# Layer 3 of a four-layer network: scores of two token tiles by seven half-size products, and gathered rows weighted by ScalarE and added by one VectorE operation

## The chip, the cores and the metric

The kernel runs on one core of a Trainium2 chip. The metric is the time of one execution on the device in microseconds, the median of three runs before the change. One execution was also taken by the hardware profiler; all times of single instructions come from that one. The core's engines are TensorE (PE; its weight loads are listed apart as PEld), VectorE (DVE), ScalarE (ACT), GpSimd (POOL) and SyncE (SP). Each works through its own instructions in order, and they wait for one another through semaphores.

## The reference, cut to what matters

Four layers work on an array x of 4 images, 512 channels and 32 × 32 = 1024 tokens each; layers 0 to 2 are attention, a channel gate and attention again. The change lies in layer 3 and in the last step of layer 2. Layer 3 looks every token up in a memory of 2048 rows of 512 values:

```python
q = jnp.transpose(x, (0, 2, 3, 1)).reshape(-1, C)     # x: normalised in groups of channels
att = q @ mempool.T                                   # 4096 tokens x 2048 rows
vals, idx = jax.lax.top_k(att, k)                     # k = 8
vals = jax.nn.softmax(vals, axis=1)
att_sparse = jnp.zeros_like(att).at[rows, idx].set(vals)
out = att_sparse @ mempool                            # sum of 8 weighted rows
x = x + out                                           # (from_tokens)
```

All is float32.

## The kernel before, in words

The tokens of layer 3 are cut into 32 tiles of 128 tokens, eight per image, in the list `tiles`. A tile passes three functions, each a step later than the one before, in the loop `for s in range(end + 3)`:

- `attention` (L1512) multiplies the tile's normalised tokens, `xn3[b]`, with the transposed memory `memT` (four blocks of 128 channels by 2048 rows). It does so in two halves of 1024 rows; each half is 8 products of 128 × 128 by 128 × 512 that add over the four channel blocks in one pair of PSUM banks, which `next_pair` hands out in turn from three. ScalarE copies each half into `att` in SBUF (L1526).
- `pick` (L1531) finds the eight largest scores (`vector.max`, shown as MAX8) and their places (`max_index`, shown as MATCH_VALUE_LOAD and FIND_INDEX8), lets GpSimd gather the eight memory rows of each token with eight indirect DMAs into `got` (128 tokens × 8 rows × 512), and makes the exponentials `et` and their sum on ScalarE. SyncE loads the tile's old x into `xr`. There are three buffers `got`, under the tags q, k and v.
- `read` (L1586) divides `et` by the sum and adds the eight weighted rows on VectorE: one `tensor_scalar_mul` (L1591) and seven `scalar_tensor_tensor` (L1593). TensorE then turns the result to channels by four transposes (L1598), into one of two PSUM banks.

`put` (L1601), a step later, adds the result to `xr` and sends it out. The last two tiles take another way, `read_last` (L1572): TensorE multiplies the gathered rows with diagonal matrices of the weights.

Instructions wrapped in `pin` keep the order in which they are written on their engine. So VectorE works, per tile, through MAX8, FIND_INDEX8, `put` of an older tile, the weights and the eight weighted additions, and GpSimd's gathers of a tile follow its FIND_INDEX8.

`prepare3` loads and normalises the next image's tokens during an image's later tiles; odd images lie in the first part of `o_full`, even ones in `xn`. `put_out2` (L1466) is the last step of layer 2 for the last image: four projections on TensorE, which stand between `attention` of tile 0 and `attention` of tile 1; VectorE adds each projection to the old x and takes its statistics, ScalarE scales the old x before that.

Layers 0 to 2 already form products by seven half-size products in `seven`, with the helpers `add7` and `sub7` (L1048), through which all their sums go.

Of the kernel before, what the change touches and what calls it, by code (L numbers as in the profile page):

```python
# [41 lines left out]
def fast_net(ctx: ExitStack, tc: tile.TileContext, a: dict, out: bass.AP, flag: bass.AP):  # L42
# [13 lines left out]
    def pin(ins):  # L56

        return tc.keep_in_program_order(ins)
# [131 lines left out]
    def tokens(src):  # L190
        return lambda k, n: src[:, k, n * NB:(n + 1) * NB]

    def project(w, rhs, m, at, evacuate, name="proj"):


        ps = place(at, f"{name}_{m}")
        for n in range(T // NB):
            for k in range(KC):
                pin(nc.tensor.matmul(  # L199
                    ps[:, n, :], w[:, k, m * P:(m + 1) * P], rhs(k, n),  # L200
                    start=(k == 0), stop=(k == KC - 1),
                ))
        evacuate(flat2(ps))
# [1259 lines left out]
        nc.vector.tensor_mul(  # L1463
            I["o"][:, m, n * NB:(n + 1) * NB], I.pop(("pv", m, n)), I.pop(("rb", m, n)))

    def put_out2(b):  # L1466
        I = img[b]
        s1 = l2[b][1]
        mv = small.tile([P, KC, 2], F32, tag="mv", name=f"mv_d{b}")

        def add_out(m, ps):
            st = small.tile([P, 2, 6], F32, tag="bnst", name=f"st_d{b}_{m}")
            for n in range(T // NB):
                xr = apool.tile([P, NB], F32, tag="xr", bufs=2, name=f"xr_c{b}_{m}_{n}")
                nc.sync.dma_start(out=xr, in_=x1[b][:, m, n * NB:(n + 1) * NB])
                pin(nc.scalar.activation(
                    xr, xr, AF.Identity, bias=I["tb"][:, m:m + 1], scale=s1[:, m:m + 1]))
                nc.vector.tensor_add(xr, ps[:, n * NB:(n + 1) * NB], xr)
                nc.sync.dma_start(out=x2[b][:, m, n * NB:(n + 1) * NB], in_=xr)
                nc.vector.bn_stats(st[:, n, :], xr)  # L1480
            nc.vector.bn_aggr(mv[:, m, :], st.rearrange("p i s -> p (i s)"))

        for m in range(KC):
            project(I["Wp"], tokens(I["o"]), m, None, lambda ps: add_out(m, ps), f"p2_{b}")
        gc3 = const.tile([P, 2, KC], F32, tag=f"gc3_{b}", name=f"gc3_{b}")
        l3[b] = (mv, gc3)

# [21 lines left out]
            ))  # L1509
            yield  # L1510

    def attention(b, tt, between=None):  # L1512

        nm = f"{b}_{tt}"
        att = eight_k([P, NI], f"att_{nm}")
        for i, (lo, hi) in enumerate(
                ((0, T), (T, T + NB), (T + NB, NI)) if (b, tt) == tiles[-1] else ((0, T), (T, NI))):
            sc = flat2(next_pair())
            for i0 in range(lo, hi, NB):
                for k in range(KC):  # L1520
                    pin(nc.tensor.matmul(  # L1521
                        sc[:, i0 - lo:i0 - lo + NB],
                        xn3[b][:, k, tt * P:(tt + 1) * P], memT[k][:, i0:i0 + NB],
                        start=(k == 0), stop=(k == KC - 1),
                    ))
            pin(nc.scalar.copy(att[:, lo:hi], sc[:, 0:hi - lo]))  # L1526
            if between is not None and i == 0:
                between()
        return att

    def pick(b, tt, att):  # L1531

        nm = f"{b}_{tt}"
        top = small.tile([P, TOPK], F32, tag="top", name=f"top_{nm}")
        if (b, tt) == tiles[-1]:
            tops = small.tile([P, 3, TOPK], F32, tag="tops", bufs=1, name="tops")
            for i, (lo, hi) in enumerate(((0, T), (T, T + NB), (T + NB, NI))):
                pin(nc.vector.max(tops[:, i, :], att[:, lo:hi]))
            pin(nc.vector.max(top, tops.rearrange("p i n -> p (i n)")))
        else:  # L1540
            pin(nc.vector.max(top, att))  # L1541
        ix = small.tile([P, TOPK], mybir.dt.uint32, tag="ix", name=f"ix_{nm}")
        pin(nc.vector.max_index(ix, top, att))
        got = big("qkv"[(b * TC + tt) % 3], f"got_{nm}").rearrange("p k (i c) -> p (k i) c", c=C)
        for i in range(TOPK):
            pin(nc.gpsimd.indirect_dma_start(  # L1546
                out=got[:, i, :], out_offset=None, in_=a["mem"],
                in_offset=bass.IndirectOffsetOnAxis(ap=ix[:, i:i + 1], axis=0),
                bounds_check=NI - 1, oob_is_err=False,
            ))  # L1550
        nmx = small.tile([P, 1], F32, tag="nmx", name=f"tmx_{nm}")
        pin(nc.vector.tensor_scalar_mul(nmx, top[:, 0:1], -1.0))  # L1552
        et = small.tile([P, TOPK], F32, tag="et", name=f"et_{nm}")
        rs = small.tile([P, 1], F32, tag="rs", name=f"trs_{nm}")
        nc.scalar.activation(et, top, AF.Exp, bias=nmx, scale=1.0, accum_out=rs)
        i = (b * TC + tt) % 3
        xr = eT_flat[:, i * NB:(i + 1) * NB].rearrange("p (k q) -> p k q", q=P)
        nc.sync.dma_start(out=xr, in_=x2[b][:, :, tt * P:(tt + 1) * P])
        return got, et, rs, xr

# [9 lines left out]
            pin(nc.scalar.activation(dg[:, i, :], ident, AF.Identity, scale=et[:, i:i + 1]))  # L1570
        return dg

    def read_last(b, tt, picked, dg):

        got, et, rs, xr = picked
        tp = next_bank().rearrange("p (k q) -> p k q", q=P)
        for i in range(TOPK):
            for m in range(KC):
                pin(nc.tensor.matmul(
                    tp[:, m, :], got[:, i, m * P:(m + 1) * P], dg[:, i, :],  # L1580
                    start=(i == 0 and m == 0), stop=(i == TOPK - 1),
                    skip_group_check=True,
                ))
        return tp, xr

    def read(b, tt, picked):  # L1586
        got, et, rs, xr = picked
        nm = f"{b}_{tt}"
        weigh(et, rs, nm)
        acc = apool.tile([P, NB], F32, tag="rb", bufs=2, name=f"acc_{nm}")  # L1590
        pin(nc.vector.tensor_scalar_mul(acc, got[:, 0, :], et[:, 0:1]))  # L1591
        for i in range(1, TOPK):
            pin(nc.vector.scalar_tensor_tensor(  # L1593
                acc, got[:, i, :], et[:, i:i + 1], acc, ALU.mult, ALU.add
            ))
        tp = next_bank().rearrange("p (k q) -> p k q", q=P)
        for m in range(KC):
            pin(nc.tensor.transpose(tp[:, m, :], acc[:, m * P:(m + 1) * P], ident))  # L1598
        return tp, xr

    def put(b, tt, done):  # L1601
        tp, xr = done
        pin(nc.vector.tensor_add(xr, tp, xr))
        nc.sync.dma_start(out=out_v[b, :, :, tt * P:(tt + 1) * P], in_=xr)
# [244 lines left out]
        places7[key] = nine[3 * i:3 * i + 3]  # L1849
    places7["Wq"] = places7["Wp"]  # L1850
    nc.gpsimd.tensor_scalar_mul(same, same, 8.0 / T)
    tiles = [(b, tt) for b in range(B) for tt in range(TC)]
    atts, picks, sums = {}, {}, {}
    scores2(0, UNITS2[0])
    for b in range(B):
# [29 lines left out]
            first7[2]()  # L1885
        apply2(b, UNITS2[-1])
        if last:
            atts[0] = attention(*tiles[0], lambda: invert2(b))
            finish2(b)
            put_out2(b)  # L1890
            continue
        over_keys(b, *UNITS2[-1][:2])
        at_border[0] = True
# [36 lines left out]
        nc.vector.tensor_scalar(  # L1930
            flag, tps[0:1, 0:1], float(2 * P * NS * B * (TC + 2 * KC)), None, ALU.not_equal)

    ahead, behind = iter(()), chain(behind, norm3(B - 1))
    end = len(tiles)
    diags = {}

    def pick_last(s):
        at = s - 1
        picks[at] = pick(*tiles[at], atts.pop(at))
        put(*tiles[s - 3], sums.pop(s - 3))  # L1940
        weigh(*picks[at][1:3], f"{tiles[at][0]}_{tiles[at][1]}")

    for s in range(end + 3):
        closing = end - 1 <= s <= end
        if closing:
            pick_last(s)
        if s < end:
            b, tt = tiles[s]
            if s > 0:
                atts[s] = attention(b, tt, (lambda: diags.update(  # L1950
                    {0: diagonals(0, picks[end - 2][1])})) if closing else None)
        if 0 <= s - 1 < end and not closing:
            picks[s - 1] = pick(*tiles[s - 1], atts.pop(s - 1))
        if s == end:
            diags[1] = diagonals(1, picks[end - 1][1])
        if s >= 3 and not closing:
            put(*tiles[s - 3], sums.pop(s - 3))
        if 0 <= s - 2 < end:
            at = s - 2
            sums[at] = (read(*tiles[at], picks.pop(at)) if at < end - 2  # L1960
                        else read_last(*tiles[at], picks.pop(at), diags[at - end + 2]))
        if s < end and tt == 2:
            ahead = prepare3(b + 1) if b + 1 < B else iter(())
        if s < end and tt >= 2:
            next(ahead, None)
        if s < end and 1 <= s <= TC:
            next(behind, None)
        if s == TC + 2:
            check_range()
        if s == TC + 4:  # L1970
            again = nc.values_load(flag, min_val=0, max_val=1)
    return again


# [702 lines left out]
```

## Time and profile before

| what | value |
|---|---|
| median of three runs | 2516.8 us (2515.85 to 2518.11) |
| the profiled execution's own time | 2516.74 us |
| its span, first to last instruction | 2514.7 us |
| TensorE busy | 2469.2 us, 98% |
| VectorE busy | 1824.1 us, 73% |
| ScalarE busy | 1026.0 us, 41% |
| GpSimd busy | 1226.5 us, 49% |
| attention of tile 1 on TensorE | 2051.7 to 2065.6 us |
| repeating part of layer 3 | 2065.7 to 2490.9 us |
| tail after the last score product | 2490.9 to 2514.7 us |

Lines of the profile are to be read so: a line of the timeline has start, duration, engine, source line, operation, output<-inputs, shapes, and in brackets how long the engine had been idle and what ended that. Consecutive instructions of one line are merged (x7). A line of windows has the stretch and its length, and then busy time and instruction count of PE, PEld, DVE, ACT and POOL, the granted clock of TensorE, and the share and rate of the DMA engines. A line of groups has count, busy time in us, mean ns of one instruction, and the idle time before.

### The profile page before, as it was taken

The numbers are of one execution on the slowest core, as the hardware profiler recorded it, in microseconds if no ns is written. First come the engines' busy times: TensorE is split into PE (matmuls) and PEld (weight loads), VectorE is DVE, ScalarE is ACT, GpSimd is POOL, SyncE is SP. The second block draws the span as 40 slices with busy tenths as digits, with TensorE's granted clock in tenths as the row PEclk, the third lists the DMA queues.
The fourth block names the chain that finished last, engine by engine and source line by source line (L and its number), as shares of the span: only waits on it lengthen the run. The fifth ranks groups of instructions, "written<-read, shape, count | busy, mean of one in ns | idle before, by whom it ended". The sixth has DMA issues, their size and how long they took to land.

```text
span 2514.7 us, 48075 instructions
## 1 busy us (share of the span) xinstructions
PE 2469.2 (98%) x18512; PEld 1171.9 (47%) x18512; DVE 1824.1 (73%) x2962; ACT 1026.0 (41%) x1245; POOL 1226.5 (49%) x1688
## 2 busy tenths in 40 slices
PE   9999999999999999999999999999999999999998
PEld 4344534555355534555633633453363344444445
DVE  5799568875788548886768677576757647887876
ACT  1567346652665336651353145125324512121212
POOL 3266425553465426554284247127405617566665
PEclk9999999999999999999999999999999999999999
DMA  2588348872698438893201230131113046667666
GB/s 85 157 229 230 111 131 224 244 215 85 176 243 232 138 89 216 238 247 125 97 30 68 103 128 18 63 116 40 55 50 134 26 135 191 214 191 219 183 188 179
DMA packets 190031, 367.19 MB, mean 146 GB/s; under 512 B 32985, under 2 KB 96473, under 8 KB 185570
## 3 DMA queue, kind: packets, MB, share of 16 engines
q1 hardware_dynamic: 109712, 186.58, 23.9%
q0 software_dynamic: 49152, 142.79, 21.0%
q10 hardware_dynamic: 30930, 34.66, 4.9%
q8 instruction: 149, 2.44, 0.4%
q14 instruction: 88, 0.72, 0.1%
HBM read 190.10 MB, written 39.58 MB: 91 GB/s over the span
## 4 chain that ended last, share of the span: by engine, by line
PE 68%; DMA 8%; issue 7%; POOL 7%; DVE 6%; ACT 3%; ACTq 0%; POOLq 0%; SPq 0%; DVEq 0%
PE pair L1121 12%; PE pair L1369 8%; PE pv L578 8%; POOL got L1546 6%; PE pair L199 6%; PE pair L513 6%; PE pair L539 5%; PE pt L471 5%; PE pt L1406 4%; PE pair L1247 4%; PE pv L1406 4%; DMA got<-in_mem,ix 4%; PE pt L767 3%; PE pair L1521 2%; ACT e L546 2%
## 5 line engine op out<-in xcount | busy, mean ns | idle before, releaser
L528 POOL DMA_DIRECT2D s<-ss x512 | 258.1, 511 | 398.2 <-issue 113.2
L552 DVE STREAM_TRANSPOSE eT<-e 128x1024 f32<-128x1024 f32 x256 | 316.4, 1236 | 161.4 <-ACT e L546 161.0
L1546 POOL DMA_INDIRECT got<-in_mem,ix x256 | 280.5, 1096 | 211.9 <-DVE tmx L1552 142.8
L1363 ACT ACTIVATE eT<-pair 128x1024 f32<-128x1024 f32 x256 | 248.5, 1022 | 312.5 <-PE pair L1369 188.9
L567 DVE BATCH_NORM_STATS2 st<-e 128x6 f32<-128x256 f32 x1024 | 350.8, 404 | 0.0
L1387 POOL TENSOR_TENSOR e<-eT 128x1024 f32<-128x1024 f32 x96 | 239.8, 2501 | 166.6 <-ACT eT L1363 122.2
L546 ACT ACTIVATE e<-pair 128x1024 f32<-128x1024 f32 x256 | 251.9, 1022 | 163.8 <-PE pair L539 122.1
L519 ACT COPY ss<-pair 128x1024 f32<-128x1024 f32 x256 | 248.9, 1019 | 85.4 <-DMA s<-ss 35.4
L513 PE MATMUL pair<-k,q 64*32 64x512 f32 x4096 | 267.3, 598 | 13.0 <-ACT e L546 13.0
L578 PEld LDWEIGHTS pv<-eT,v 128*64 128x64 f32 x4096 | 221.1, 137 | 71.6 <-issue 55.2
L578 PE MATMUL pv<-eT,v 128*64 128x128 f32 x4096 | 250.0, 275 | 4.1 <-ACT pv L638 4.1
L1369 PE MATMUL pair<-q,k 64*128 64x512 f32 x1024 | 240.0, 605 | 2.0 <-DVE sum L1048 0.9
L1388 DVE TENSOR_TENSOR eT<-eT,e 128x1024 f32<-128x1024 f32 x96 | 144.7, 1508 | 130.1 <-POOL e L1387 129.9
L539 PE MATMUL pair<-s,wmix 32*32 32x512 f32 x4096 | 160.6, 600 | 3.4 <-DMA s<-ss 1.9
L1593 DVE SCALAR_TENSOR_TENSOR acc<-got,et,acc 128x512 f32<-128x512 f32 x210 | 157.9, 752 | 7.5
L1383 POOL TENSOR_TENSOR eT<-eT 128x1024 f32<-128x1024 f32 x32 | 83.4, 2605 | 161.1 <-ACT eT L1363 156.2
L1369 PEld LDWEIGHTS pair<-q,k 64*128 64x128 f32 x1024 | 92.3, 186 | 140.2 <-issue 66.6
L1526 ACT COPY att<-pair 128x1024 f32<-128x1024 f32 (+1 forms) x65 | 64.9, 999 | 216.4 <-PE pair L1521 216.3
L513 PEld LDWEIGHTS pair<-k,q 64*32 64x32 f32 x4096 | 57.1, 105 | 178.6 <-ACT e L546 84.1
L1048 DVE TENSOR_TENSOR k<-k,pair 128x512 f32<-128x512 f32 (+1 forms) x96 | 78.1, 857 | 66.5 <-PE pair L1121 52.8
L651 POOL TENSOR_TENSOR o<-pv,rb 64x256 f32<-64x256 f32 x128 | 118.9, 929 | 6.4
L1541 DVE MAX8 top<-att 128x8 f32<-128x2048 f32 x31 | 71.1, 2293 | 70.0 <-ACT att L1526 70.0
(383 smaller groups left out, 3745.2 us busy)
## 6 DMA issues: line engine op xcount, KB each, us to landing
s<-ss SPq DMA_DIRECT2D x512, 128.0 KB
s<-ss POOLq DMA_DIRECT2D x512, 128.0 KB, 4.4
rb<-r POOLq DMA_DIRECT2D x64, 128.0 KB, 6.0
o<-o SPq DMA_DIRECT2D x32, 256.0 KB
xr_c<-x SPq DMA_DIRECT2D x32, 256.0 KB
rb_c<-r SPq DMA_DIRECT2D x64, 128.0 KB
eT<-x SPq DMA_DIRECT2D x32, 256.0 KB
out<-eT SPq DMA_DIRECT2D x32, 256.0 KB
```

Source lines behind the costliest of these rows:

```text
L513: pin(nc.tensor.matmul(sc[m * NS:(m + 1) * NS, r, :], q[r * HD:(r + 1) * HD, m, s * NS:(s + 1) * NS], k_[r * HD:(r + 1) * HD, m, n * NB:(n ...
L519: pin(nc.scalar.copy(ss[:, :, n * NB:(n + 1) * NB], sc))
L528: pin(relays[side].dma_start(out=s2[2 * m + r::NH], in_=ss[m * NS:(m + 1) * NS, r, :]))
L539: pin(nc.tensor.matmul(mixed(s, r // 2)[t * NS:(t + 1) * NS, r % 2, :].rearrange("p (qq k) -> p qq k", qq=2), wmix[r * NS:(r + 1) * NS], s ...
L546: pin(nc.scalar.activation(e[:, half].rearrange("p r qq k -> p (r qq k)"), flat2(mixed(s, half)), AF.Exp))
L552: pin(nc.vector.transpose(eT[:, j % 2].rearrange("p b (qq i r) x -> p i r qq b x", qq=2, i=4)[:, i, 2 * half:2 * half + 2], e[:, half].rea ...
L567: pin(nc.vector.bn_stats(st[:, i, 2 * half + r, qq, :], e[:, half, r, qq, :]))
L578: pin(nc.tensor.matmul(pv[r * HD:(r + 1) * HD, gp, :], I["v"][:, t, g * HD:(g + 1) * HD], eT[:, j % 2, t, :, 4 * g:4 * g + 4], start=(t == ...
L1121: pin(nc.tensor.matmul(ps[:, m, :], w[:, k, m * P:(m + 1) * P], x[:, k, :], start=(k == 0), stop=(k == 1)))
L1363: pin(nc.scalar.activation(e, scs[len(es)], AF.Exp, scale=SCALE))
L1369: pin(nc.tensor.matmul(sc[:, r, :], I["k"][r * HD:(r + 1) * HD, m, t * P:(t + 1) * P], I["q"][r * HD:(r + 1) * HD, m, n * NB:(n + 1) * NB] ...
L1546: pin(nc.gpsimd.indirect_dma_start(out=got[:, i, :], out_offset=None, in_=a["mem"], in_offset=bass.IndirectOffsetOnAxis(ap=ix[:, i:i + 1], ...
```

## The change

The tiles of an image are taken in pairs, tokens tt and tt + 4 (`tiles` is reordered). For a pair, the scores are a matrix of 2 × 2 blocks: two tiles by two halves of the memory, over two halves of the channels. `two_tiles` makes them by seven products of half the channels each, 28 multiplications of 128 × 128 by 128 × 512 in place of 32. Three of the results add in PSUM onto an earlier one after ScalarE has copied that out; three are added to `att` by VectorE. The products need sums of memory blocks, `memory_sums`, made once on VectorE during `put_out2`, and sums of token blocks, `token_sums`, made for each pair. This is done for tiles 2 to 29; tiles 0, 1, 30 and 31 go by `attention` as before.

The weighted sum is divided: ScalarE multiplies each gathered row in place by its weight (`weigh_rows`, in two groups of four rows), `add_up` adds the eight rows by one `tensor_reduce` over a view in which the row index runs innermost, and `turn_back` transposes. Of tiles n, n+1 computed in a pass of the loop, those picked earlier, n-3 and n-2, are added up and put in that pass. `xr` moves from `eT_flat`, which now holds the sums of the memory, to four places in `e`. The score buffers are chosen by `att_at`.

```diff
-    def put_out2(b):
+    def put_out2(b, between):
...
             project(I["Wp"], tokens(I["o"]), m, None, lambda ps: add_out(m, ps), f"p2_{b}")
+            next(between)
...
+    mem_t = [eT_flat[:, i * NI:(i + 1) * NI].rearrange("p (k q) -> p k q", k=2) for i in range(4)]
+
+    def memory_sums():
...
+        t1, t2, t3, t4 = ([t[:, k, :] for k in range(2)] for t in mem_t)
+        for out, x, y in ((t1, raw(0, 1), raw(0, 0)), (t2, raw(1, 1), t1),
+                          (t3, raw(1, 1), raw(0, 1)), (t4, raw(1, 0), t2)):
+            for part in zip(out, x, y):
+                sub7(*part)
+            yield
...
+    def token_sums(n):
...
+        a11, a12, a21, a22 = token_blocks(n)
+        s1, s2, s3, s4 = token_places
+        sub7(s3, a11, a21)
+        add7(s1, a21, a22)
+        sub7(s2, s1, a11)
+
+    def two_tiles(n):
...
+        x, z, y = (next_pair() for _ in range(3))
+        next_pair()
+        sub7(s4, a12, s2)
...
+        for ps, start, a_, b_, use, to in (
+                (x, True, a11, raw(0, 0), "=", one[:, left]),
+                (z, True, s3, of(2), "=", other[:, right]),
+                (x, False, s2, of(1), "=", other[:, left]),
+                (z, False, a22, of(3), "+", other[:, left]),
+                (x, False, s1, of(0), "+", other[:, right]),
+                (y, True, a12, raw(1, 0), "+", one[:, left]),
+                (x, False, s4, raw(1, 1), "=", one[:, right])):
+            for c in range(2):
+                for k in range(2):
+                    pin(nc.tensor.matmul(
+                        ps[:, c, :], a_[:, k, :], b_(k, c),
+                        start=(start and k == 0), stop=(k == 1), skip_group_check=True))
+            if use == "=":
+                pin(nc.scalar.copy(to, flat2(ps)))
+            elif ps is not y:
+                add7(to, to, flat2(ps))
+            yield other
+            if ps is y:
+                last = lambda: add7(one[:, left], one[:, left], flat2(y))
+        last()
+        yield one
...
-        i = (b * TC + tt) % 3
-        xr = eT_flat[:, i * NB:(i + 1) * NB].rearrange("p (k q) -> p k q", q=P)
+        xr = spare[:, n % 4 * NB:(n % 4 + 1) * NB].rearrange("p (k q) -> p k q", q=P)
...
-    def read(b, tt, picked):
...
-        weigh(et, rs, nm)
-        acc = apool.tile([P, NB], F32, tag="rb", bufs=2, name=f"acc_{nm}")
-        pin(nc.vector.tensor_scalar_mul(acc, got[:, 0, :], et[:, 0:1]))
-        for i in range(1, TOPK):
-            pin(nc.vector.scalar_tensor_tensor(
-                acc, got[:, i, :], et[:, i:i + 1], acc, ALU.mult, ALU.add
-            ))
+    def ready(n, picked):
...
+        pin(nc.vector.reciprocal(ri, rs))
+        pin(nc.scalar.activation(et, et, AF.Identity, scale=ri))
+
+    def weigh_rows(picked, lo, hi):
+        got, et, rs, xr = picked
+        for i in range(lo, hi):
+            pin(nc.scalar.activation(
+                got[:, i, :], got[:, i, :], AF.Identity, scale=et[:, i:i + 1]))
+
+    def add_up(n, picked):
+        got, et, rs, xr = picked
+        acc = apool.tile([P, NB], F32, tag="rb", bufs=2, name=f"acc_{n}")
+        pin(nc.vector.tensor_reduce(acc, got.rearrange("p i c -> p c i"), AX.X, ALU.add))
+        return acc, xr
...
-    tiles = [(b, tt) for b in range(B) for tt in range(TC)]
+    tiles = [(b, t) for b in range(B) for tt in range(TC // 2) for t in (tt + 4, tt)]
...
+    for n in range(2, end - 2, 2):
+        b, j = tiles[n][0], n // 2 % (TC // 2)
+        parts = two_tiles(n)
+        if n > 2:
+            weigh_rows(picks[n - 3], 4, TOPK)
+        next(parts)
+        weigh_rows(picks[n - 2], 0, 4)
+        picks[n - 1] = pick(n - 1, atts.pop(n - 1))
...
+        if n > 2:
+            add_tile(n - 3)
+        next(parts)
+        weigh_rows(picks[n - 2], 4, TOPK)
+        next(parts)
...
+        add_tile(n - 2)
+        next(parts)
+        if n > 2:
+            turn_tile(n - 3)
...
+        atts[n] = next(parts)
+        turn_tile(n - 2)
...
+        ready(n - 1, picks[n - 1])
+        weigh_rows(picks[n - 1], 0, 4)
+        next(parts)
+        picks[n] = pick(n, atts.pop(n))
+        next(parts)
+        atts[n + 1] = next(parts)
+        if n + 2 < end - 2:
+            token_sums(n + 2)
+        ready(n, picks[n])
+        if n > 2:
+            put_tile(n - 3)
+        put_tile(n - 2)
...
+    def between():
+        turn_tile(s - 3)
+        weigh_rows(picks[s - 2], 0, TOPK)
+
+    atts[s] = attention(s, between, (att_at[0] + 2) % 3)
```

In the diff the products are numbered from 1 to 7 in the order of the list in `two_tiles`; "product 5" is `(x, False, s1, of(0), ...)`. After the loop the tail takes tiles 27, 28 and 29 by `add_up` and tiles 30 and 31 by `read_last`.

## The prediction

> **What bounds the kernel now.** I read the first part of the page, then the windows of the last stage, then its timeline engine by engine, the groups, and at the end the timeline of the tail. The page and three stretches (attention(1) alone, the repeating part of layer 3, the tail):
>
> ```profile
> PE 2469.2 (98%) x18512; PEld 1171.9 (47%) x18512; DVE 1824.1 (73%) x2962; ACT 1026.0 (41%) x1245; POOL 1226.5 (49%) x1688
> 2051.90:2065.70 13.80, 13.80 (x35) 6.15 (x35) 7.36 (x9) 3.07 (x6) 2.42 (x3) 1.00 0.70 232
> 2065.70:2490.90 425.20, 425.20 (x1082) 194.15 (x1082) 346.67 (x453) 89.13 (x143) 271.60 (x252) 1.00 0.67 196
> 2490.90:2514.70 23.80, 16.04 (x133) 15.04 (x131) 6.61 (x12) 3.42 (x11) 10.44 (x11) 0.97 0.58 168
> ```
>
> The columns after the length are PE, PEld, DVE, ACT, POOL. In the repeating part TensorE has no gap, at full clock, so it is the bound; VectorE is next with 82%. One tile on VectorE, and the gathers that its FIND_INDEX8 releases on GpSimd:
>
> ```profile
> 2151.75 2.29 DVE L1541 MAX8 top<-att 128x8 f32<-128x2048 f32 x1 [2.21 <-ACT att L1526]
> 2154.08 0.09 DVE L1543 MATCH_VALUE_LOAD ix<-top,att 128x8 f32 x1
> 2154.16 2.29 DVE L1543 FIND_INDEX8 ix<-top,att 128x8 uint32<-128x2048 f32 x1
> 2156.36 0.14 DVE L1552 TENSOR_SCALAR tmx<-top 128x1 f32<-128x1 f32 x1
> 2156.41 0.68 DVE L1603 TENSOR_TENSOR eT<-pv,eT 128x512 f32<-128x512 f32 x1
> ...
> 2158.23 5.48 DVE L1593 SCALAR_TENSOR_TENSOR acc<-got,et,acc 128x512 f32<-128x512 f32 x7
> 2165.92 2.29 DVE L1541 MAX8 top<-att 128x8 f32<-128x2048 f32 x1 [2.21 <-ACT att L1526]
> ```
>
> ```profile
> 2156.71 0.99 POOL L1546 DMA_INDIRECT got<-in_mem,ix  x1 [3.18 <-DVE tmx L1552]
> 2158.01 1.06 POOL L1546 DMA_INDIRECT got<-in_mem,ix  x1 [0.30 <-issue]
> ...
> 2166.71 1.00 POOL L1546 DMA_INDIRECT got<-in_mem,ix  x1 [0.30 <-issue]
> ```
>
> A tile takes 14.17 us (2151.75 to 2165.92), a pair of tiles 28.34. TensorE fills it with 16 products of 0.858 (two tiles' halves of 8 follow each other every 6.87) and 0.44 for four transposes. VectorE works 11.96 and waits 2.21. The eight gathers start 1.30 apart, 1.57 while the SCALAR_TENSOR_TENSOR chain runs (10.0 from first to last), and the chain of work shows 3.9 from issue to landing.
>
> VectorE reductions from the first stage, the only ones that tell something of the new `add_up`:
>
> ```profile
> 39.98 0.27 DVE L836 TENSOR_REDUCE of_head<-ident 128x8 f32<-128x128 f32 x1
> 40.18 0.36 DVE L822 TENSOR_REDUCE mask<-ident 128x32 f32<-128x128 f32 x1
> 40.57 0.23 DVE L839 TENSOR_SCALAR same<-mask 128x128 f32<-128x128 f32 x1
> ```
>
> Both read the same 128 elements. L836 reads runs of 4 neighbours; L822 (the view `p (t x) -> p x t`) jumps 32 elements between any two reads. The exact durations are 272 and 357 ns.
>
> [...] (128x1024 additions from PSUM took 1215 ns[...]; the 128x1024 reduction L901 1221). [...] L822 against L836[...]: 85 ns more for 128 elements, 0.66 ns each. The number of results does not explain it: L1423, with 16 results from 512 elements, took 658 ns[...].
>
> **The change, part by part, for a pair of tiles (14 of them, tiles 2 to 29).**
> TensorE: 28 half-size products instead of 32: 28 × 0.858 + 0.88 for transposes = 24.9; 3.4 less.
> ScalarE: four copies of 1.01, 16 weighings of 128x512 (two of L1476 run in 1.52, so 0.71 apart, 0.81 the last) 11.4, exponentials and scales 1.6: 17.0 of a pair. It has room, but it is in order, and the evacuation of product 3, which product 5 needs before it may add to the same PSUM, stands behind the weighing of rows 4 to 7.
> GpSimd: the same 16 gathers, 20.8 at 1.30. The dependent chain on one tile's FIND is priced under the first rival.
> VectorE: removed are eight weighings per tile (0.52 + 5.48, with the scaling of `et` 0.5: 13.0 a pair). What stands there now:
> - MAX8 to `tmx`, 4.66 (2151.75 to 2156.41), twice: 9.3
> - three additions of 128x1024 at 1.215: 3.65
> - four token sums of 128x256 at 0.415: 1.66
> - two `put` at 0.6 and two reciprocals at 0.19: 1.6
> - two `add_up`, each 4096 elements, the next read always 512 elements (2 KB) on.
> So 16.2 + 2r, r being one `add_up`. The trace has no reduction of this size or stride. [...] From the nearest row, L822: 4.4 + 4096 × 0.66 ns = 7.1. I take 7.1, because it is the one measured strided read[...]. Nothing in the trace says that the penalty ends with short rows.
> With it VectorE needs 16.2 + 14.2 = 30.4, call it 30.3 with starts that overlap by 0.07, against 28.34 now and TensorE's 24.9. VectorE becomes the bound and TensorE waits in two places: the transposes of tile n-2 for its `add_up`, product 7 for the addition of product 5.
> Done once: eight subtractions of 128x1024 for `mem_t`, 9.8 on VectorE during `put_out2`. VectorE has some 4 us free in each of four projections of 6.87, so six are hidden; the last two (2.4) come after the last projection and delay tile 0's MAX8, under attention(1). Token loads, `xr` and `prepare3` keep their sizes and queues; `xr` only moves to `e`. No cost.
>
> **The sum, in times of the profiled execution.** `put_out2` ends on TensorE at 2051.8; VectorE finishes its statistics and two subtractions at 2057.3, tile 0's FIND at 2061.9; last gather issued 0.3 + 9.1 later, landed 2075.2, weighed 2076.0; `add_up` of tile 0 ends 2083.1, the two additions 2085.6. From there 13 pairs × 30.3 = 393.9: 2479.5. The tail, all on VectorE: FIND of tile 28 and the last addition and `put`s 2486.9; FIND 29 2491.6; `add_up` 27 and 28 2505.7; FIND 30 and small ones 2511.6; `add_up` of 29, whose weighing ScalarE ends at 2513.1 (it starts after the first evacuation of attention(31)), 2520.3; `put` and the last tile's maxima and FIND (5.05 as at 2489.90 now) 2526.0; gather 2526.3. Now:
>
> ```profile
> 2489.90 2.48 DVE L1538 MAX8 tops<-att 128x8 f32<-128x1024 f32 x3
> ...
> 2494.92 0.13 DVE L1552 TENSOR_SCALAR tmx<-top 128x1 f32<-128x1 f32 x1
> ...
> 2509.44 0.69 DVE L1603 TENSOR_TENSOR eT<-pt,eT 128x512 f32<-128x512 f32 x1 [10.10 <-PE pt L1579]
> ```
>
> The first gather of the last tile starts at 2495.27, 19.4 before the end of the span (2514.7). Unchanged, this gives a span of 2545.7, and with the 2.0 around the span (2516.74 − 2514.7) 2547.8. The profiled execution lies at the median (2516.8), so nothing is corrected: **2548 us**. One more microsecond of r costs about 29: twice 13 pairs, three in the tail.
>
> **Rivals.**
> - Strides cost nothing, r = 4.4 (0.32). Then VectorE needs 25.0 and TensorE 24.9 and neither sets the pair. The chain does: FIND of tile n, 0.3, 9.1 to 10.0 for the gathers, 3.9 landing, 0.85 for the last weighing, `add_up` 4.4, two additions 2.4, reciprocal, MAX8 and FIND 4.8: 25.8 to 26.7. With 26.2, start and tail worked out as above: gather of the last tile at 2469, end 2489, **2492** (2485 to 2500). This is the case on the other side. It decides at r = 6.0, 0.39 ns an element; half the penalty that L822 shows would be under it. For it: L836, L901[...]; against it: L822.
> - [...]r = 8.7 (0.15): 2548 + 1.6 × 29 = **2594**.
> - Half the penalty, r 5.2 to 6.4 (0.10): 2495 to 2528, either sign.
> - The saving arrives whole (0.03, within the first in sign): gathers hidden, TensorE stays the bound at 24.9, 48 us less and some 5 lost in the tail: 2474. Against it is the chain above, which does not fit into 24.9.
> That the seven products are not fewer is excluded: their count follows from the code. Accumulating into PSUM while the other pair is evacuated adds a wait only if ScalarE is late, which 17.0 of 30 does not make it in the forecast.
>
> **How the numbers follow.** r near 7.1: 0.40, likeliest; its own range, r from 6.5 to 7.8, is 2530 to 2568. Faster by over 0.2% (5 us, about what a measurement tells from no change): the first and fourth rival and a third of the half penalty, 0.38; within 0.2%: 0.04; slower: 0.58. For 8 in 10 the range must reach both signs: from 2488, leaving 0.07 below (the whole saving and the lower end of r = 4.4), to 2580[...].
>
> **What would show it.** The group of `add_up` with a mean near 7.1 us; VectorE over 95% busy in the repeating part, TensorE near 82%; MAX8 of tiles n two apart at 30.3; TensorE's idle time put down to `acc` and `att` from VectorE; weighings at 0.7; 4.66 from MAX8 to `tmx`. A mean of 4.4 proves the main step wrong, and then VectorE should idle before the second `add_up` of a pair, waiting for ScalarE's row 7. A longer landing than 3.9, or gathers slowed beyond 1.57, would lengthen the first rival's pair too.

## The result, and the profile after

| | before | changed |
|---|---|---|
| median | 2518.11 us (2515.85 to 2522.76, 5 runs) | 2558.51 us (2552.81 to 2559.94, 5 runs) |
| ratio to before, 95% interval | | 1.0159 (1.0145 to 1.0174) |
| profiled execution, span | 2516.74, 2514.7 us | 2552.81, 2551.1 us |

The change makes the kernel 1.6% slower. The first part of its page, and the windows of the 13 regular pairs and of the tail (stretch, length, then PE, PEld, DVE, ACT, POOL, the granted clock, the share and rate of the DMA engines):

```profile
PE 2448.7 (96%) x18400; PEld 1157.2 (45%) x18400; DVE 1930.3 (76%) x2828; ACT 1183.0 (46%) x1515; POOL 1202.4 (47%) x1688
2091.00:2480.00 389.00, 343.31 (x836) 151.55 (x835) 383.85 (x271) 212.39 (x349) 210.20 (x213) 0.97 0.61 185
2490.00:2551.00 61.00, 40.77 (x185) 27.27 (x183) 32.95 (x24) 18.49 (x43) 25.65 (x26) 0.89 0.52 153
```

VectorE is busy for 383.85 of 389.00 us, 98.7%; before it was TensorE that had no gap. One pair on VectorE, from its timeline:

```profile
2213.04 2.28 DVE L1618 MAX8 top<-att 128x8 f32<-128x2048 f32 x1
...
2217.69 7.28 DVE L1678 TENSOR_REDUCE acc<-got 128x512 f32<-128x4096 f32 x1
...
2224.95 7.23 DVE L1678 TENSOR_REDUCE acc<-got 128x512 f32<-128x4096 f32 x1
2232.11 2.33 DVE L1048 TENSOR_TENSOR att<-att,pair 128x1024 f32<-128x1024 f32 x2
...
2234.48 2.29 DVE L1618 MAX8 top<-att 128x8 f32<-128x2048 f32 x1
```

The two reductions take 14.5 of the 30.0 us between this MAX8 and the one that starts at 2243.03, two on. Over 13 pairs the mean is 30.04, against 28.38 before. The page's groups for the reduction and for ScalarE's weighing, and, from the waits between 2090 and 2480, what TensorE waits for (total, times, longest):

```profile
L1678 DVE TENSOR_REDUCE acc<-got 128x512 f32<-128x4096 f32 x30 | 215.5, 7200 | 20.4 <-ACT got L1672 20.3
L1672 ACT ACTIVATE got<-got,et 128x512 f32<-128x512 f32 x240 | 159.1, 715 | 37.7 <-DMA got<-in_mem,ix 37.1
```

```profile
PEld pv L1685 <- DVE acc L1678: 34.3, 12, 3.8
PEld pt L1685 <- DVE acc L1678: 21.7, 11, 3.4
```

TensorE waits at the transposes for VectorE's sums. Of the 36.4 us that the span grew, by the starts of MAX8 and FIND_INDEX8 in the two timelines: the start of tile 0's MAX8 moved by -1.3 (2057.14 to 2055.82); from there to tile 29's MAX8 21.0 more (406.6 to 427.7); from there to the last tile's FIND_INDEX8 16.0 more (28.95 to 44.96); the rest 0.7 more. So over two fifths of the loss is in the tail. VectorE's tail and the ScalarE work that it waits for, from their timelines:

```profile
2499.28 7.10 DVE L1678 TENSOR_REDUCE acc<-got 128x512 f32<-128x4096 f32 x1 [3.90 <-ACT got L1672]
...
2517.94 7.08 DVE L1678 TENSOR_REDUCE acc<-got 128x512 f32<-128x4096 f32 x1 [5.91 <-ACT got L1672]
...
2530.66 0.13 DVE L1629 TENSOR_SCALAR tmx<-top 128x1 f32<-128x1 f32 x1
```

```profile
2511.07 0.30 ACT L1632 ACTIVATE et<-top,tmx 128x8 f32<-128x8 f32 x1 [11.82 <-DVE tmx L1629]
...
2512.01 0.99 ACT L1534 COPY att<-pair 128x1024 f32<-128x1024 f32 x1
2512.90 5.00 ACT L1672 ACTIVATE got<-got,et 128x512 f32<-128x512 f32 x8
```

VectorE's idle time is in brackets. ScalarE stood idle for 11.8 us at the exponential of tile 30, behind which the weighing of tile 29 is queued.

### The profile page after: what moved, and what is told of

It is laid out like the page before. It is cut to its first block, busy times and chain, and to the rows that moved or that the text cites. A ratio compares the mean times of both kernels' runs of the same rounds, so it can differ in the third digit from the quotient of the medians.

```text
span 2551.1 us, 47898 instructions
## 1 busy us (share of the span) xinstructions
PE 2448.7 (96%) x18400; PEld 1157.2 (45%) x18400; DVE 1930.3 (76%) x2828; ACT 1183.0 (46%) x1515; POOL 1202.4 (47%) x1688
## 4 chain that ended last, share of the span: by engine, by line
PE 68%; DVE 10%; issue 8%; DMA 7%; ACT 4%; POOL 3%; ACTq 0%; SPq 0%; POOLq 0%; DVEq 0%
PE pair L1121 12%; PE pair L1369 8%; PE pv L578 8%; PE pair L513 6%; PE pair L539 5%; PE pair L199 5%; PE pt L471 5%; PE pt L1406 4%; PE pair L1247 4%; PE pv L1406 4%; PE pt L767 3%; DMA got<-in_mem,ix 3%; DVE acc L1678 2%; POOL got L1623 2%; ACT e L546 2%
## 5 line engine op out<-in xcount | busy, mean ns | idle before, releaser
L1623 POOL DMA_INDIRECT got<-in_mem,ix x256 | 257.3, 1005 | 276.5 <-ACT et L1632 133.3
L1678 DVE TENSOR_REDUCE acc<-got 128x512 f32<-128x4096 f32 x30 | 215.5, 7200 | 20.4 <-ACT got L1672 20.3
L1594 PE MATMUL pair<-eT,tokens 128*128 128x512 f32 x448 | 200.3, 595 | 3.7 <-ACT att L1598 3.3
L1672 ACT ACTIVATE got<-got,et 128x512 f32<-128x512 f32 x240 | 159.1, 715 | 37.7 <-DMA got<-in_mem,ix 37.1
L1594 PEld LDWEIGHTS pair<-eT,tokens 128*128 128x128 f32 x448 | 84.0, 190 | 107.0 <-issue 99.2
```

Source lines behind the costliest of these rows:

```text
L1594: pin(nc.tensor.matmul(ps[:, c, :], a_[:, k, :], b_(k, c), start=(start and k == 0), stop=(k == 1), skip_group_check=True))
L1623: pin(nc.gpsimd.indirect_dma_start(out=got[:, i, :], out_offset=None, in_=a["mem"], in_offset=bass.IndirectOffsetOnAxis(ap=ix[:, i:i + 1], ...
L1678: pin(nc.vector.tensor_reduce(acc, got.rearrange("p i c -> p c i"), AX.X, ALU.add))
```

## The experiments

The theory is the prediction's: a strided `add_up` of 7.1 to 7.2 us makes VectorE the bound of a pair. Its rivals: the stride isn't what makes it long; or something else would hold the pair just as long, above all the chain gather, ScalarE, VectorE. The first four runs followed from these, the others from what the first showed. "Pair" is the mean distance between the MAX8 of tiles two apart.

### The same reduction over neighbours

```diff
-        pin(nc.vector.tensor_reduce(acc, got.rearrange("p i c -> p c i"), AX.X, ALU.add))
+        pin(nc.vector.tensor_reduce(
+            acc, got.rearrange("p i c -> p (i c)").rearrange("p (c i) -> p c i", i=TOPK), AX.X, ALU.add))
```

It adds eight neighbours within a row, so the sum over the eight rows is left out; all else is the same work.

> The one tensor_reduce of the changed kernel reads the same 4096 values of got in the order in which they lie (eight neighbours make one sum); everything else stays. The sum of the eight rows is left out by that: the values added are the wrong ones, the work is the same but for the jump. Theory (the jump costs 0.68 ns an element and VectorE is the bound): one add_up falls from 7.20 to 4.4 us, a pair from 30.0 to 25.8 to 26.7, the time to 2485 to 2500. Rival (the operation is slow for its size, or because ScalarE and the gathers write into got beside it): add_up stays at 7 us and the time over 2545.

Measured: 2513.7 us (2505.3 to 2517.3), ratio to before 0.998 (0.9971 to 0.999). The reduction took 4.42 us, 2.8 less. The stride is what makes it long. But the gain is 45 us, not the 2.8 × 29 = 81 that VectorE alone would give, and the time lies 14 us above the range expected: the pair is 27.45. A timeline of one pair (GpSimd issuing the last gather of a tile, ScalarE weighing that row, VectorE's second reduction), and what TensorE waits for between 2100 and 2440:

```profile
2238.06 0.99 POOL L1623 DMA_INDIRECT got<-in_mem,ix  x1 [0.30 <-issue]
...
2245.21 0.72 ACT L1672 ACTIVATE got<-got,et 128x512 f32<-128x512 f32 x1 [0.87 <-DMA got<-in_mem,ix]
...
2245.96 4.42 DVE L1678 TENSOR_REDUCE acc<-got 128x512 f32<-128x4096 f32 x1 [4.98 <-ACT got L1672]
```

```profile
PEld pair L1594 <- ACT att L1598: 34.5, 25, 4.1
```

The row is weighed 7.2 us after its gather was issued, and VectorE has waited 5.0 us for it. TensorE now waits for evacuations, which stand on ScalarE behind weighings whose rows have not landed. This is the chain of the first rival, longer than it was priced.

### Three additions in place of the reduction

```diff
-        pin(nc.vector.tensor_reduce(acc, got.rearrange("p i c -> p c i"), AX.X, ALU.add))
+        add7(got[:, 0:4, :], got[:, 0:4, :], got[:, 4:8, :])
+        add7(got[:, 0:2, :], got[:, 0:2, :], got[:, 2:4, :])
+        add7(acc, got[:, 0, :], got[:, 1, :])
```

> The eight rows are added by three additions of 2048, 1024 and 512 contiguous elements in place of the one reduction; the output is the reference's. Theory: 2.29 + 1.22 + 0.69 = 4.2 us for a tile, some 0.1 more where one waits for the other; a pair 25.6 to 26.6, the time 2480 to 2500, under the kernel before. Within that: if TensorE becomes the bound again a pair takes 24.9 and the time is 2475; if the chain from one tile's FIND over its gathers to its sum is the bound, 25.8 or more, with VectorE idle before the first addition, released by ScalarE. Rival (VectorE is slowed on got by what else writes there): the three take 6.5 us or more, the time over 2540.

Measured: 2523.6 us (2518.1 to 2531.9), ratio 1.0025 (1.0015 to 1.0035), pair 28.36. The additions take 3.54 and 0.69, 4.2 us together, less than the reduction over neighbours; the time is 10 us longer all the same, and 24 above the range expected. The timeline shows a gather beside the additions:

```profile
2301.07 3.54 DVE L1048 TENSOR_TENSOR got<-got 128x2048 f32<-128x2048 f32 x2
2301.26 2.97 POOL L1623 DMA_INDIRECT got<-in_mem,ix  x1 [0.30 <-issue]
```

That issue takes 2.97 us where others take 1.00. It is the seventh of the eight gathers of a tile whose last row the second additions of the pair then wait for, 3.73 us at 2309.07; so it lies in the chain that bounds this kernel.

### The scores of the change, the weighing of before

```diff
     def weigh_rows(picked, lo, hi):
-        for i in range(lo, hi):
-            pin(nc.scalar.activation(
-                got[:, i, :], got[:, i, :], AF.Identity, scale=et[:, i:i + 1]))
+        return
...
-        pin(nc.vector.tensor_reduce(acc, got.rearrange("p i c -> p c i"), AX.X, ALU.add))
+        pin(nc.vector.tensor_scalar_mul(acc, got[:, 0, :], et[:, 0:1]))
+        for i in range(1, TOPK):
+            pin(nc.vector.scalar_tensor_tensor(
+                acc, got[:, i, :], et[:, i:i + 1], acc, ALU.mult, ALU.add
+            ))
```

> The seven products alone: rows are weighted and added by VectorE with one product and seven fused products as before, ScalarE's weighing is gone; the order of tiles and everything else as in the changed kernel. Theory: VectorE has 16.2 + 2 x 6.2 = 28.6 us for a pair and stays the bound, 28.6 to 29.2 against 30.0: 2530 to 2545. Rival (the seven products bring waits of their own, TensorE for evacuations and accumulations): a pair stays at 30 and the time at 2555 or more. If VectorE were not the bound, 2500 or less.

Measured: 2503.4 us (2500.0 to 2505.7), ratio 0.9937 (0.9917 to 0.9958): faster than before, and 55 us faster than the change. The expectation missed by some 27 us. The pair is 27.38: VectorE's eight operations of a tile occupy 5.91 us (2429.35 to 2435.26), less than the one strided reduction of 7.2 alone, and they need no weighing by ScalarE. And from MAX8 of tile 29 to the last FIND_INDEX8 it needs 31.5 us, not 45.0. So the seven products do gain time; the new weighing loses it.

### Where the stride begins to cost

To the changed kernel, at its end, reductions of the same 4096 elements by groups of eight were added, with growing steps between one element and the next (every form twice; the core of the edit):

```diff
+        pin(nc.vector.tensor_reduce(
+            res[rep].rearrange("p (g s) -> p g s", s=4),
+            flat.rearrange("p (g i s) -> p g s i", i=TOPK, s=4), AX.X, ALU.add))
```

> The changed kernel with nine more reductions, twice over, on VectorE after the last tile, on a tile of ones that GpSimd fills: 4096 elements in groups of eight that lie 1, 2, 4, 8, 32, 128 and 512 elements apart, then 2048 elements in groups of eight that lie 256 apart, and in groups of four that lie 512 apart. Their results are used by nothing. Theory[...]: 4.4 us for 1 and 2 apart, some 7.1 from 4 apart on, and 3.6 for each of the two with 2048 elements. Rival (a far jump pays more than a near one): rising from 4 to 512 apart. Rival (the operation is slow for its size): 7 us at any distance.

The timeline, of one run; the lines shown have steps of 1, 2, 4, 8, 32 and 512 elements:

```profile
2544.44 4.41 DVE L2135 TENSOR_REDUCE res<-rows 128x512 f32<-128x4096 f32 x1
2548.88 4.42 DVE L2137 TENSOR_REDUCE res<-rows 128x512 f32<-128x4096 f32 x1
2553.34 7.40 DVE L2140 TENSOR_REDUCE res<-rows 128x512 f32<-128x4096 f32 x1
2560.77 7.47 DVE L2143 TENSOR_REDUCE res<-rows 128x512 f32<-128x4096 f32 x1
2568.28 7.03 DVE L2146 TENSOR_REDUCE res<-rows 128x512 f32<-128x4096 f32 x1
...
2582.41 7.03 DVE L2152 TENSOR_REDUCE res<-rows 128x512 f32<-128x4096 f32 x1
```

A step of 8 bytes cost nothing (4.42 us against 4.41), one of 16 bytes 3.0 us for 4096 elements (7.40), one of 32 bytes 3.1 (7.47), and those of 128 bytes and of 2 KB 2.6 (7.03 each); the second time round each form took the same. With half the elements, 1 KB apart, it is half the time (3.59). The differences come to 0.64 to 0.75 ns for an element. That the cost would begin at 16 bytes was the author's assumption, which no trace had shown before this run.

### Both ways of weighing, a tile each

The runs above leave VectorE too much work (7.2, or 5.9 per tile) or the chain too long (4.2 to 4.4). Here the tile that is added second, n-2, goes by VectorE's eight operations, which take each row as it lands (at 2074.51 and 2075.93 of this run one of them waited 0.47 and 0.66 us for its row), and the tile n-3, whose rows landed long before, by ScalarE and three additions. (The first `if` stands in `weigh_rows`, the second in `add_up`.)

```diff
+    def by_vector(n):
+        return n % 2 == 0 or n == len(tiles) - 3
...
+        if by_vector(n):
+            return
...
-        pin(nc.vector.tensor_reduce(acc, got.rearrange("p i c -> p c i"), AX.X, ALU.add))
+        if by_vector(n):
+            pin(nc.vector.tensor_scalar_mul(acc, got[:, 0, :], et[:, 0:1]))
+            for i in range(1, TOPK):
+                pin(nc.vector.scalar_tensor_tensor(
+                    acc, got[:, i, :], et[:, i:i + 1], acc, ALU.mult, ALU.add))
+            return acc, xr
+        add7(got[:, 0:4, :], got[:, 0:4, :], got[:, 4:8, :])
+        add7(got[:, 0:2, :], got[:, 0:2, :], got[:, 2:4, :])
+        add7(acc, got[:, 0, :], got[:, 1, :])
```

> As the changed kernel, but the tile of each pair that is added second (n-2, and tile 29) is weighted and added by VectorE's eight fused products as before the change, 5.9 us, and the other tile (n-3) is weighed by ScalarE and added by three additions of neighbours (2048, 1024 and 512 results), 4.2 us. VectorE then has 26.5 - 5.9 + 4.2 = 24.8 us a pair, TensorE 24.9. Theory (what held the version with neighbours at 27.45 a pair was that the tile added second needs gather, landing, ScalarE's weighing and one whole addition one after another; fused products take each row as it lands): pair 25.5 to 26.5, 2503 - 13 x (0.9 to 1.9) = 2478 to 2491. Rival (the gathers of the second tile, issued slowly beside a long addition and landing late, bound the pair whoever weighs): pair 27.4 or more, VectorE idle at the second tile's rows, 2500 or more.

Measured: 2479.6 us (2477.0 to 2482.5), ratio 0.9858 (0.9842 to 0.9875), pair 25.62: as the theory had it, and faster than both kernels. The windows:

```profile
2100.00:2440.00 340.00, 333.50 (x856) 151.46 (x855) 333.98 (x395) 144.82 (x246) 248.56 (x218) 1.00 0.74 216
```

TensorE and VectorE are both busy for 98%.

### Shorter additions

The mixed kernel with three additions of 1024 results in place of 2048 and 1024:

```diff
-        add7(got[:, 0:4, :], got[:, 0:4, :], got[:, 4:8, :])
-        add7(got[:, 0:2, :], got[:, 0:2, :], got[:, 2:4, :])
+        add7(got[:, 0:2, :], got[:, 0:2, :], got[:, 2:4, :])
+        add7(got[:, 0:2, :], got[:, 0:2, :], got[:, 4:6, :])
+        add7(got[:, 0:2, :], got[:, 0:2, :], got[:, 6:8, :])
```

> As the mixed kernel, with the 2048-result addition cut into two of 1024 (so three additions of 1024 and one of 512, together 4.4 us). If GpSimd's gather issue is held for as long as a VectorE addition with both inputs in SBUF runs, the issues beside the additions take up to 2.2 us, not 3.0, and the time is within 5 us of the mixed kernel. If the hold has to do with the length of a single addition, the slow issues vanish (1.0 to 1.3 us).

Measured: 2485.0 us (2482.0 to 2489.1), ratio 0.9881 (0.9865 to 0.9898), pair 25.89. The first two additions, then the third, and the three issues beside them:

```profile
2200.20 2.54 DVE L1048 TENSOR_TENSOR got<-got 128x1024 f32<-128x1024 f32 x2
...
2202.84 1.23 DVE L1048 TENSOR_TENSOR got<-got 128x1024 f32<-128x1024 f32 x1
```

```profile
2200.38 1.90 POOL L1623 DMA_INDIRECT got<-in_mem,ix  x1 [0.30 <-issue]
2202.59 1.02 POOL L1623 DMA_INDIRECT got<-in_mem,ix  x1 [0.30 <-issue]
2203.91 1.03 POOL L1623 DMA_INDIRECT got<-in_mem,ix  x1 [0.30 <-issue]
```

The slow issue shrinks to 1.90 us, and the next two take 1.02 and 1.03. They are short because they begin late: at 2202.59 the second addition has 0.15 us left (to 2202.74), at 2203.91 the third has 0.16 (to 2204.07). Each issue ends 0.87 us after the addition beside which it began. So the first reading of the expectation holds: an issue waits for the end of the addition that runs when it starts. Shortening this wait gained nothing here; the 0.33 us more of additions a pair, 14 pairs, is most of the 5.4 us that this kernel is slower than the mixed one.

### The one operation, swapped in the mixed kernel

```diff
-        add7(got[:, 0:4, :], got[:, 0:4, :], got[:, 4:8, :])
-        add7(got[:, 0:2, :], got[:, 0:2, :], got[:, 2:4, :])
-        add7(acc, got[:, 0, :], got[:, 1, :])
+        pin(nc.vector.tensor_reduce(acc, got.rearrange("p i c -> p c i"), AX.X, ALU.add))
```

> As the mixed kernel, with the strided reduction of the changed kernel in place of the three additions, for the tile of each pair that ScalarE weighs. Nothing else differs. Theory (VectorE's total work sets the pair, so each us more in its reduction costs a us a pair): 7.2 - 4.2 = 3.0 more, pair 25.6 + 3.0 = 28.6, 14 pairs, 2479.6 + 14 x 3.0 = 2521, within 2514 to 2527. Rival (a chain through gathers and landings sets the pair, and VectorE's idle time takes up part of the 3.0; the gathers are issued 2 us faster without the long addition beside them): pair 26.5 to 27.7, 2492 to 2510.

Measured: 2525.5 us (2518.3 to 2528.3), ratio 1.0027 (1.0018 to 1.0036), pair 28.60 (28.6 expected). Against the mixed kernel 45.9 us more for 14 reductions that are each 3.0 longer (42; in the runs beside this one the kernel before was 2.4 longer too), and VectorE still 98% busy (366.09 of 372.00 us from 2093 to 2465):

```profile
2093.00:2465.00 372.00, 332.09 (x838) 147.27 (x837) 366.09 (x362) 146.33 (x248) 223.91 (x213) 1.00 0.64 194
```

The 3.0 us in this one operation cost 2.98 in a pair (28.60 − 25.62), as the prediction's sum has it.

### The new weighing alone, in the old order

The kernel before, with this in `read`:

```diff
-        pin(nc.vector.tensor_scalar_mul(acc, got[:, 0, :], et[:, 0:1]))
-        for i in range(1, TOPK):
-            pin(nc.vector.scalar_tensor_tensor(
-                acc, got[:, i, :], et[:, i:i + 1], acc, ALU.mult, ALU.add
-            ))
+        for i in range(TOPK):
+            pin(nc.scalar.activation(
+                got[:, i, :], got[:, i, :], AF.Identity, scale=et[:, i:i + 1]))
+        pin(nc.vector.tensor_reduce(acc, got.rearrange("p i c -> p c i"), AX.X, ALU.add))
```

> The kernel before, its scores and its order, with ScalarE weighing the eight rows in place and the one strided reduction in place of VectorE's eight fused products. VectorE has per tile 4.66 + 7.2 + some 1.2 = 13.1 us, TensorE 14.17 a tile. Theory (the reduction's 2.8 us too many cost time only where VectorE is the bound; here TensorE still is): 2512 to 2524, TensorE over 97% busy. Rival (weighing in ScalarE's order, between the evacuations of the scores, and the reduction that can only start after the last row, delay the evacuations and so TensorE): over 2530.

Measured: 2692.5 us (2687.6 to 2695.1), ratio 1.0694 (1.0676 to 1.0712). The theory's 2512 to 2524 is missed by some 170 us. The timelines of VectorE and ScalarE:

```profile
2205.36 2.28 DVE L1541 MAX8 top<-att 128x8 f32<-128x2048 f32 x1
...
2218.20 7.12 DVE L1594 TENSOR_REDUCE acc<-got 128x512 f32<-128x4096 f32 x1 [7.17 <-ACT got L1592]
2225.23 2.29 DVE L1541 MAX8 top<-att 128x8 f32<-128x2048 f32 x1
```

```profile
2211.06 2.56 ACT L1592 ACTIVATE got<-got,et 128x512 f32<-128x512 f32 x4 [0.48 <-DVE et L1564]
```

In this order the weights of tile s-2 are scaled by VectorE behind MAX8 and FIND_INDEX8 of tile s-1, the weighing waits for them, the reduction for the weighing, and the next MAX8 for the reduction: 5.4 to the scaling, 0.3, 7.1 of weighing with a copy in between, 7.0 of reduction, 19.9 us a tile in series. Work that was one engine's became a chain over two. The run thus says nothing on the reduction's length, so the next one was made.

### The new weighing alone, in the changed kernel's order

The changed kernel, with the scores of a pair by four halves of 8 full products and ScalarE's copy, no `token_sums`, no additions to `att`; `turn_tile(n - 2)` one half later. (The core; `memory_sums` stays.)

```diff
+        def half(att, t, i, sc):
+            for c in range(2):
+                for k in range(KC):
+                    pin(nc.tensor.matmul(
+                        sc[:, c, :], xn3[tiles[n][0]][:, k, t * P:(t + 1) * P],
+                        memT[k][:, i * T + c * NB:i * T + (c + 1) * NB],
+                        start=(k == 0), stop=(k == KC - 1)))
+            pin(nc.scalar.copy(att[:, i * T:(i + 1) * T], flat2(sc)))
```

> The changed kernel with its pipeline a tile later, its weighing by ScalarE and its strided reduction, but the scores of a pair by 32 full products as before the change (two tiles of two halves, no sums of tokens, no additions to the scores; the transposes of tile n-2 stand one half later). TensorE 28.3 us a pair; VectorE 29.6 - 3.6 - 2.0 = 24.0. Theory (the slow reduction costs nothing where VectorE has room, and what went wrong with the new weighing alone in the old order was the order: exponential, weighing and reduction of consecutive tiles in series): pair 28.3 to 28.8, the tail some 5 longer, 2515 to 2530. Rival (weighing in place blocks evacuations or gathers in this order too): pair over 30, 2545 or more.

Measured: 2548.4 us (2544.8 to 2549.6), ratio 1.0123 (1.0106 to 1.014). Ten of the 13 pairs take 28.34 or 28.35 us, TensorE's own time, with two reductions of 7.2 in each: there the slow operation costs nothing, because VectorE has room (87% busy from 2100 to 2440). The time, 18 us above the range expected, is lost elsewhere. Three pairs are 34.89, 30.06 and 30.60 (10.5 us more); in each of them TensorE stands idle before transposes, for 4.51, 1.32 and 2.04 us, but why in these three stays open. And from tile 29's MAX8 to the last FIND_INDEX8 it is 45.65 us against 28.95 before (16.7 more), where the expectation had 5; there VectorE waits 4.57 and 5.90 us for rows that ScalarE weighs, as in the change.

### The tail by VectorE

The changed kernel, with tiles 28 and 29 alone weighted and added by VectorE's eight operations (`by_vector` of the mixed kernel, true for these two).

> The changed kernel, with tiles 28 and 29 alone (the two that are added up in the tail after the loop, besides 27) weighted and added by VectorE's eight fused products, 5.9 us each, as before the change; tiles 0 to 27 unchanged. Theory (the tail's ScalarE order costs 3.9 us of waiting ahead of the 28th reduction and 5.9 ahead of the 29th, and each reduction is 1.3 longer than the fused products): from MAX8 of tile 29 to FIND_INDEX8 of the last tile 32.7 as in the mixed strided kernel, in place of 45.0; pair unchanged at 30.0; 2558.5 - 12.3 = 2546, within 2541 to 2551. Rival (the wait only moves, to the landing of the rows or to the transposes): less than 5 us gained, 2553 or more.

Measured: 2547.8 us (2545.5 to 2550.1), ratio 1.0118 (1.0091 to 1.0144). From tile 29's MAX8 to the last FIND_INDEX8 32.7 us (2493.19 to 2525.91), the number expected, in place of 45.0; the median is 10.7 lower. The pairs stay at 30.09. So 12.2 us of the change's loss (44.96 − 32.72) come from how two tiles in the tail are weighted: 9.8 us of waiting for ScalarE, and the rest because the reduction is longer.

## Why the prediction was right, and where not

The forecast was 2548 us, slower because a strided `add_up` makes VectorE the bound; 2558.5 was measured, and in the pairs this reason holds. In the tail a second one came in that the sum had all but left out: waits for ScalarE.

- **`add_up` at 7.1, from L822 and L836.** Right: 7.20 in the mean. With a 4.4 for a reduction without a stride, the two short reductions of the first stage gave the duration to 2%. The stride run shows that the step alone makes the difference, at long rows and at every step tried from 16 bytes to 2 KB (7.03 to 7.47 us, against 4.41 and 4.42 below that). That 4.4, from which the first rival starts too, was the author's estimate; a straight line through L836 (128 elements in 272 ns) and L901 (1024 in 1221) gives 4.5 for 4096 elements and 679 ns for the 512 of L1423, above its 658, so the argument on the number of results holds without it. The 8.7 of the second rival, of whose 0.15 the range leaves out 0.13, was the author's estimate too, and nothing in the traces showed it.
- **The pair at 30.3, VectorE as the bound, over 95% busy.** Right: 30.04 and 98.7%; the swap in the mixed kernel shows that it is the reduction's length that sets it. Two small errors nearly cancel: from the starts in the pair shown, the two reductions take 14.4 us, not 14.2, and all else 15.6, not 16.2, since most instructions begin some 0.08 before the one ahead of them ends, and the sum took off 0.1 in all. TensorE waits at the transposes of tile n-2, as named. It shows 88% rather than 82% busy; the granted clock of 0.97 over 389 us, from products that run slower (below), makes about half of that, and the rest is open.
- **The start.** Right: the first `add_up` starts at 2075.43 (2076.0 predicted).
- **The tail to the first gather of the last tile, 2526.3.** Mis-sized: 2531.5. The 13 pairs ended 3.2 early (the last two additions at 2476.3, not 2479.5). From there the tail took 8.4 longer than summed, and two waits are all of it: `add_up` of 28 waited 3.90 for ScalarE's rows, where the sum had no wait, and that of 29 waited 5.91, where it had 1.5. The weighing of tile 29 ended at 2517.9, not 2513.1: it stood behind the exponential of tile 30, which needs VectorE's FIND_INDEX8, and the copy after it. The prediction counted the evacuation ahead of that weighing and not the exponential. That the last tile's gather comes only 5.2 late is in part luck: the early pairs hid 3.2 of the 8.4.
- **From the span to the median.** 2545.7 and 2.0 were taken together; the profiled execution took 2552.8 against 2547.8 predicted, and the median lies a further 5.7 above it, where for the kernel before the two agreed. Tile 0's MAX8, behind layers whose code is the same in both, started at 2055.8 in the change's profile and at 2065.2 in that of the tail run, so such a difference can arise before layer 3; that it did in the other four runs is not shown, and stays open.
- **First rival, strides at no cost: pair 25.8 to 26.7, 2492.** Mis-sized: with the reduction over neighbours the pair is 27.45 and the time 2513.7. The terms that failed are the landing, taken as 3.9 from the chain of work (7.2 from issue to weighing in the pair shown), and, again, the tail (39.6 us from tile 29's MAX8 to the last FIND_INDEX8, 28.95 before). "A wait only if ScalarE is late" was also the case here: evacuations stood behind rows that hadn't landed. With so short an `add_up` the change gains 0.2%, not the rival's 1%.
- **What the whole saving is worth.** Of the 3.4 us of TensorE a pair, 2.8 show once VectorE is relieved and the chain cut: a pair of 25.62 against 28.38, and 36 us less than before (2479.6 against 2515.9 beside it).

## What to carry to other kernels

Before one operation replaces a chain of several, price it with the access pattern that it really has: here eight fused operations (5.9 us) were shorter than one reduction whose elements lie 2 KB apart (7.2). A step given to another in-order engine must be priced as a chain, with what stands ahead of it in that engine's order; in the tail, where nothing else covers it, every such wait shows (3.90 and 5.91 us here). Where two engines are near their bound, splitting one kind of work between them tile by tile (one each, 2479.6 us) gave more than moving all of it (2523.6) or leaving all of it (2503.4).

## What the runs showed of the hardware that was not expected

**TensorE ran at half its clock after some pauses.** From the changed kernel's tail:

```profile
2506.44 1.12 PE L1685 MATMUL pv<-ident,acc 128*128 128x128 f32 x4 [3.47 <-DVE acc L1678]
2507.35 3.12 PE L1529 MATMUL pair<-memT,eT 128*128 128x512 f32 x4
2510.31 1.88 PE L1529 MATMUL pair<-eT 128*128 128x512 f32 x4
```

```profile
2507.00:2508.00 1.00, 1.00 (x4) 0.69 (x3) 1.00 (x1) 0.00 (x0) 0.00 (x0) 0.50 0.00 0
```

After 3.47 us without work, four MATMUL records, which are two products, take 3.12 us, at a granted clock of 0.50, and the four after them 1.88. The slow stretch lasts 3.41 us. It also came after a shorter pause, of 2.56 us:

```profile
2202.24 0.78 PE L1685 MATMUL pt<-ident,acc 128*128 128x128 f32 x4 [2.56 <-DVE acc L1678]
2202.81 5.21 PE L1594 MATMUL pair<-eT 128*128 128x512 f32 x8
2207.86 3.60 PE L1594 MATMUL pair<-eT,tokens 128*128 128x512 f32 x8
```

```profile
2202.70:2206.00 3.30, 3.30 (x6) 1.46 (x5) 3.30 (x4) 1.35 (x3) 0.00 (x0) 0.50 0.00 0
```

The repeating part has twelve pauses of 2.56 to 2.95 us at the transposes; after seven of them the clock was halved for 3.41 us, after five it was not, and their lengths don't tell the two apart. A wait at TensorE can thus cost more than its length: the eight records above took 5.21 us, the eight after them 3.60. What it came to in the end is not shown.

**VectorE's additions held up the gathers.** An issue took 2.97 us beside an addition of 2048 results and 1.90 beside one of 1024, both with their two inputs in SBUF, and 1.00 beside the reductions, strided or not, and beside the additions to `att`, which read one input from PSUM (12 of 14 in the changed kernel; 1.02 and 1.15 in the others). What counts is how much of the addition is left when the issue starts: in the runs with three additions, with shorter ones and in the mixed one, issues longer than 1.01 us beside the additions of rows ended 0.87 to 0.89 us after the end of the addition, whatever they took. What in an issue waits isn't shown.

**A gather waited for ScalarE where rows are scaled in place.** In the changed kernel a tile's first gather starts 0.85 us after `tmx`, behind the exponential; in the kernel before, and in the one with the old weighing, it waits for `tmx` alone (0.35 before). With the new weighing in the old order it is 0.84 again. So the weighing in place brings the wait; whether it needs to isn't shown.
